# A factorization layer on one core: the 4x2x3 scheme for two more outer products, a fourth output tile and output sums by adding DMAs

## The chip, the cores and the metric

The kernel runs on one core of one Trainium2 chip. The metric is device time in microseconds of one execution, from inputs in HBM to the output in HBM. Shown are the median and the range of several executions, and one execution that the hardware profiler recorded.

## The reference

`x` is 1024 x 512, `weight` is 64 x 512 x 512 (embedding e, feature f, model column m), all in float32.

```
out_lin = x @ lin_w.T + lin_b
xv = einsum('bf,efm->bem', x, weight)
zp = einsum('bf,efm->bem', square(x), square(weight))
y  = out_lin + 0.5 * sum(square(xv) - zp, axis=1)     # sum over e
```

Nearly all of the work is `xv`: a matrix product of 1024 x 512 by 512 x 32768, whose results are squared and summed over e. The sum of `zp` over e is x squared times the sum over e of the squared weights, one small matrix product at the end.

## The kernel before, in words

**Groups.** The 512 model columns are cut into 22 groups, two of 16 columns and twenty of 24 (a "full group"). Each group is one matrix product of 1024 x 512 by 512 x (24 x 64).

**Outer products.** A group is computed by the Strassen-Winograd scheme of 2x2 blocks: seven outer products, numbered 1 to 7, instead of eight. Their left sides (sums of blocks of x) stay in the tiles X1 to X7 for the whole run. Their right sides are blocks of the group's weights, `w11`, `w12`, `w21`, `w22`, and sums of them in `T1` and `T2`. These sums and two more into `w12` and `w21` are made by adding DMAs: four per group, each of 768 KB in a full group, issued by GpSimd (`dma_add`, L342). `w22` and `T1` have two copies, for even and odd groups. The plain weight loads are issued by SP, twelve of 384 KB per full group.

**Inner products.** Each outer product is split once more: into 7 inner products of 384 columns, each in two halves of rows, 14 in all (`tree`), or, for those in `HK`, into 20 products of 256 columns by a scheme for 4x2x3 blocks (`wide_tree`). The sums of weights that these need are made by GpSimd into `t0` to `t2`. The inner products go to four pairs of PSUM banks, `b1`, `b3`, `b2_0`, `b2_1`. ScalarE copies a partial result from pair to pair (`copy`, L319), so that later products accumulate onto it; VectorE and GpSimd (`tt`, L309) bring results into the output tiles `oa`, `ob`, `c`. ScalarE squares finished outputs (L326) and VectorE sums them over e into `acc` (L335).

**Output sums.** Outer product 1 goes to `oa`; 6 gives `ob = oa + P6`; 2 is added to `oa`, which is then finished; 7 gives `oa = ob + P7`; 4 gives `c = oa + P4`, finished; 5 is added to both `oa` and `ob`, each of its results twice, and `oa` is finished; 3 is added to `ob`, which is finished.

**Order.** The program is a list of operations, each with the engines that may run it, a cost on each, and the operations whose data or buffers it needs. A planner (`Plan.order`) plays that list once, with latest times counted back from TensorE's work, and so fixes the order of every engine's queue; each engine then runs its queue strictly in order. In the plan an adding DMA costs GpSimd 1 us, lands a fixed time after that, and then takes up SP for its cost:

```
cost = 2.9 * rows / 1024
plan.add({POOL: 1.0}, emit, reads + writes, writes + (token,), land=cost + 2.5)
plan.add({SP: cost}, None, (token,), ())
```

## Time and profile before

| | |
|---|---|
| median of 3 executions | 1427.72 us (1426.12 to 1429.38) |
| the profiled execution's own span, first to last instruction | 1425.4 us (2.3 us under the median) |
| TensorE, VectorE, GpSimd, ScalarE busy | 99%, 79%, 77%, 51% |
| granted TensorE clock | 1.000 |
| matmul instructions | 4680: two for each product of the code |
| DMA | 184.53 MB, mean 129 GB/s |

In the rows of the profile PE is TensorE, PEld its weight loads, DVE VectorE, ACT ScalarE and POOL GpSimd. A row of instruction groups reads: line, engine, operation, output tile <- input tiles, shapes, count | busy us, mean ns of one | idle time of the engine just before them and what ended it. Buffer numbers are left out of names, so X1 to X7 all read X, and `w` is w11, w12 or w21. A row of DMA queues gives packets, MB and the share of 16 DMA engines' time; a row of DMA issues gives the queue that issues, the count, KB each and the median us from issue to landing. In rows of stretches the busy time of each engine and its count are followed by the granted clock, the DMA share and GB/s.

### The profile page before, as it was taken

The numbers are of one execution on the slowest core, as the hardware profiler recorded it, in microseconds if no ns is written. First come the engines' busy times: TensorE is split into PE (matmuls) and PEld (weight loads), VectorE is DVE, ScalarE is ACT, GpSimd is POOL, SyncE is SP. The second block draws the span as 40 slices with busy tenths as digits, with TensorE's granted clock in tenths as the row PEclk, the third lists the DMA queues.
The fourth block names the chain that finished last, engine by engine and source line by source line (L and its number), as shares of the span: only waits on it lengthen the run. The fifth ranks groups of instructions, "written<-read, shape, count | busy, mean of one in ns | idle before, by whom it ended". The sixth has DMA issues, their size and how long they took to land.

```text
span 1425.4 us, 14830 instructions
## 1 busy us (share of the span) xinstructions
PE 1407.8 (99%) x4680; PEld 883.2 (62%) x4680; DVE 1123.7 (79%) x1365; ACT 731.2 (51%) x1048; POOL 1093.3 (77%) x895
## 2 busy tenths in 40 slices
PE   8999999999999999999999999999999999999998
PEld 3887565666656566665656566665656666565653
DVE  2678778796977879697887879687787969778875
ACT  2446545463645646464554646465464646455431
POOL 7897869696787869687776968787686968878670
PEclk9999999999999999999999999999999999999999
DMA  7667636464653646465463645555364646545241
GB/s 237 183 142 177 150 84 160 116 142 109 141 130 95 163 89 162 102 138 135 109 155 86 156 118 133 125 125 136 89 166 102 156 104 143 129 99 133 67 131 61
DMA packets 78893, 184.53 MB, mean 129 GB/s; under 512 B 28064, under 2 KB 29088, under 8 KB 78816
## 3 DMA queue, kind: packets, MB, share of 16 engines
q1 hardware_dynamic: 65488, 115.17, 27.5%
q0 software_dynamic: 12752, 67.38, 25.1%
q10 hardware_dynamic: 576, 1.05, 0.2%
q8 instruction: 38, 0.62, 0.2%
q14 instruction: 39, 0.32, 0.1%
HBM read 127.04 MB, written 6.19 MB: 93 GB/s over the span
## 4 chain that ended last, share of the span: by engine, by line
PE 91%; DVE 6%; issue 1%; DMA 1%; POOL 1%; ACT 0%; SPq 0%; DVEq 0%; POOLq 0%
PE b L356 75%; PE b_r L356 6%; PE b_l L356 6%; DVE acc L335 1%; DVE ob L309 1%; PE b_l L393 1%; DVE oa L309 1%; PE b_r L393 1%; PE b_l L813 1%; PE b_r L813 1%; DVE p L309 1%; DVE w_sum L335 1%; DMA X<-xT 1%; DVE c L309 0%; DMA ob<-lin_wT 0%
## 5 line engine op out<-in xcount | busy, mean ns | idle before, releaser
L356 PE MATMUL b<-t,X 128*128 128x384 f32 (+1 forms) x2144 | 720.9, 476 | 5.1 <-DVE oa L309 3.3
L356 PEld LDWEIGHTS b<-t,X 128*128 128x128 f32 x2144 | 403.2, 190 | 266.9 <-issue 23.2
L356 PE MATMUL b<-w,X 128*128 128x384 f32 (+1 forms) x816 | 276.1, 474 | 0.0
L309 POOL TENSOR_TENSOR t<-w 128x768 f32<-128x768 f32 (+1 forms) x128 | 182.4, 1431 | 119.7 <-PE b_l L356 104.4
L326 ACT ACTIVATE oa<-oa 128x768 f32<-128x768 f32 (+1 forms) x176 | 144.6, 824 | 201.6 <-DVE oa L309 182.9
L356 PEld LDWEIGHTS b<-w,X 128*128 128x128 f32 x816 | 154.6, 190 | 98.3 <-ACT p L319 13.0
L319 ACT COPY p<-b 128x768 f32<-128x768 f32 (+1 forms) x158 | 122.3, 774 | 173.4 <-PE b L356 173.2
L335 DVE TENSOR_REDUCE acc<-oa 128x12 f32<-128x768 f32 (+1 forms) x176 | 158.6, 921 | 39.9 <-ACT oa L326 39.8
L335 DVE TENSOR_REDUCE w_sum<-wsq 128x12 f32<-128x768 f32 (+1 forms) x176 | 158.6, 921 | 27.7 <-ACT wsq L326 27.7
L309 POOL TENSOR_TENSOR t<-w,t 128x384 f32<-128x384 f32 (+1 forms) x136 | 141.9, 1043 | 4.9
L319 ACT COPY b<-b 128x768 f32<-128x768 f32 (+1 forms) x134 | 102.5, 765 | 74.7 <-PE b L356 70.1
L309 DVE TENSOR_TENSOR oa<-b,oa 128x768 f32<-128x768 f32 (+1 forms) x66 | 61.3, 929 | 86.1 <-PE b L356 86.1
L326 ACT ACTIVATE wsq<-w 128x768 f32<-128x768 f32 (+1 forms) x132 | 104.9, 823 | 46.8 <-DMA w<-weight 31.8
L309 POOL TENSOR_TENSOR ob<-ob,p 128x768 f32<-128x768 f32 (+1 forms) x44 | 78.8, 1791 | 22.9 <-DVE p L309 22.9
L326 ACT ACTIVATE c<-c 128x768 f32<-128x768 f32 (+1 forms) x88 | 70.4, 819 | 47.9 <-DVE c L309 46.6
L356 PE MATMUL b<-T,X 128*128 128x384 f32 (+1 forms) x264 | 92.3, 476 | 0.0
L309 POOL TENSOR_TENSOR t<-t,w 128x256 f32<-128x256 f32 (+1 forms) x80 | 90.2, 1202 | 0.0
L309 DVE TENSOR_TENSOR ob<-b,oa 128x768 f32<-128x768 f32 (+1 forms) x66 | 61.3, 929 | 30.0 <-PE b L356 30.0
L309 DVE TENSOR_TENSOR p<-b,p 128x768 f32<-128x768 f32 (+1 forms) x88 | 81.5, 926 | 1.1 <-ACT wsq L326 0.6
L326 ACT ACTIVATE ob<-ob 128x768 f32<-128x768 f32 (+1 forms) x88 | 71.0, 826 | 21.6 <-DVE ob L309 14.6
L309 DVE TENSOR_TENSOR oa<-oa,b 128x768 f32<-128x768 f32 (+1 forms) x88 | 81.2, 923 | 0.8
L309 DVE TENSOR_TENSOR ob<-ob,b 128x768 f32<-128x768 f32 (+1 forms) x88 | 80.0, 926 | 2.0 <-PE b L356 1.4
(118 smaller groups left out, 2130.8 us busy)
## 6 DMA issues: line engine op xcount, KB each, us to landing
w<-weight SPq DMA_DIRECT2D x120, 384.0 KB, 3.5
T<-weight SPq DMA_DIRECT2D x40, 384.0 KB, 4.2
w<-T POOLq DMA_DIRECT2D x20, 768.0 KB, 5.8
T1a<-weight SPq DMA_DIRECT2D x20, 384.0 KB, 3.7
w22a<-weight SPq DMA_DIRECT2D x20, 384.0 KB, 3.2
T1a<-weight POOLq DMA_DIRECT2D x10, 768.0 KB, 7.9
T<-T1a POOLq DMA_DIRECT2D x10, 768.0 KB, 7.5
T1b<-weight SPq DMA_DIRECT2D x20, 384.0 KB, 4.5
```

The costliest lines, as they stand in the source:

```text
L309: return f(o.ap, a.ap, b.ap)
L319: return nc.scalar.copy(o.ap, i.ap)
L326: lambda _: nc.scalar.activation(o.ap, i.ap, AF.Square), i.atoms, o.atoms)
L335: nc.vector.tensor_reduce(o, x, axis=AX.X, op=ALU.add)
L356: nc.tensor.matmul(a.ap, b.ap, w.ap, start=start, stop=True, skip_group_check=True)
L393: nc.tensor.matmul(o[j].ap, x.ap[:, ts((g * 2 + j) % (NB // 2), P)], w.ap, start=(k == 0), stop=(k == NK - 1),)
L813: nc.tensor.matmul(z.ap, view(xe[h, k // KH])[:, k % KH, ts((g * 2 + j) % (NB // 2), P)], reg("w2_sum", k * M, M).ap, start=(k == 0), stop ...
```

## The change

- The 4x2x3 scheme is used for outer products 1, 6 and 7 (`HK`) in full groups, where only 1 had it. Its sums are written in another form, with seven operations on GpSimd instead of eight.
- There is a fourth output tile, `od`; `c` is now `oc`. Outer product 5 goes to `od` alone, 7 to `oc`, 2 to `oa`, 3 to `ob`, 4 to `oc`. After outer product 7 the new function `outer_out` issues four adding DMAs: `ob += od` in two halves of rows and then `od += oc` in two halves; `od` is then finished.
- The order of outer products is 1 6 5 7 2 3 4.
- In 6, 7, 2, 3 and 4 (`EARLY`), the result P5 of `tree` is added to the output as soon as it is there, and no copy of it is kept.
- The three buffers for sums become one space `t` that is filled in turn; the bias uses `od` at the start; the last stage uses other tiles.
- The planner plays the list 24 times; after each time `blame` raises the urgency of what TensorE waited for, and the time with the earliest end is taken. An adding DMA's cost in the plan is 2.4 instead of 2.9 per 1024 elements.

```diff
-ORDER = (1, 6, 2, 7, 4, 5, 3)
-HK = (1,)
+ORDER = (1, 6, 5, 7, 2, 3, 4)
+HK = (1, 6, 7)
+EARLY = (6, 7, 2, 3, 4)
...
+    def order(self):
+        boost, best = defaultdict(float), None
...
+        for _ in range(ROUNDS):
+            done = self.schedule(boost)
+            end = max(o.end for o, e in done if e == PE)
...
+            if best is None or end < best[0]:
+                best = end, done
+            self.blame(done, boost)
+        return best[1]
+
+    def blame(self, done, boost):
...
+        for o, e in done:
+            if e != PE:
+                continue
+            lost = o.end - o.costs[PE] - free
+            free = o.end
+            if lost < 0.05:
+                continue
+            x = slowest(o)
+            for _ in range(CHAIN):
+                if x is None or x.engine == PE:
+                    break
...
+                boost[x.n] += PUSH * max(lost, 0.2)
...
-            o.latest = latest
+            o.latest = latest - boost[o.n]
...
-    make("oa", 4 * WIDE)
-    make("ob", 4 * WIDE)
-    make("c", 4 * WIDE)
+    for o in ("oa", "ob", "oc", "od"):
+        make(o, 4 * WIDE)
...
-        cost = 2.9 * rows / 1024
+        cost = 2.4 * rows / 1024
         plan.add({POOL: 1.0}, emit, reads + writes, writes + (token,), land=cost + 2.5)
         plan.add({SP: cost}, None, (token,), ())
...
+    def outer_out(g):
+        iw = GROUPS[g] // 2 * E
+        for o, i in (("ob", "od"), ("od", "oc")):
+            for k in range(2):
+                x, y = (reg(z, 2 * k * WIDE, iw, (WIDE, 2)) for z in (o, i))
+                dma_add(x.ap, y.ap, 2 * iw, y.atoms, x.atoms)
+        for m in range(4):
+            finish(g, 5, reg("od", m * WIDE, iw), m, 0)
...
-    ADDEND = {6: "oa", 2: "oa", 7: "ob", 4: "oa", 3: "ob"}
-    TARGET = {1: "oa", 6: "ob", 2: "oa", 7: "oa", 3: "ob", 4: "c"}
+    ADDEND = {6: "oa", 2: "oa", 7: "ob", 4: "oc", 3: "ob"}
+    TARGET = {1: "oa", 6: "ob", 5: "od", 2: "oa", 7: "oc", 3: "ob", 4: "oc"}
...
         product(5, "b3", True)
-        copy(small(p5), whole("b3"))
+        if i in EARLY:
+            leave(3, "b3")
+        else:
+            copy(small(p5), whole("b3"))
         product(3, "b3", False)
...
+            if i == 7:
+                outer_out(g)
```

Three places in the queues, each from a full group in the middle of the run. First GpSimd's queue before, from the sum into w21, which outer product 4 needs, to the sum into w12 for the next group; t0 to t2 are the sums of weights, DMA rows are the adding DMAs, and the words in brackets are the semaphores that the row waits for (DMASW: an adding DMA, DMAHW: a load).

```order
L346 DMA w21_71<-T2_76 128x1536 [waits PE_49]
L309 TENSOR_TENSOR t0_80<-T1a_74 128x2x384 [waits PE_49]
L309 TENSOR_TENSOR oa_77<-p5_0_83,oa_77 128x2x384 [waits DVE_49,Pool_49]
...
L346 DMA T2_76<-T1b_75 128x1536 [waits DMAHW6_49,DMAHW5_49,DMASW4_49]
L309 TENSOR_TENSOR t1_81<-w22a_72,t1_81 128x384 [waits Pool_49]
L309 TENSOR_TENSOR oa_77<-oa_77,ob_78 128x2x384 [waits DVE_49]
...
L346 DMA w12_70<-w22b_73 128x1536 [waits DMAHW4_49,DMAHW7_49,DMAHW0_49,Activation_49]
```

Between the first two adds stand eight operations on tiles, between the second and third five; no two adds are neighbours. Now the same queue of the change, from behind outer product 7's last sums to the first sum for outer product 4 (t from w21):

```order
L403 DMA ob_78<-od_80 128x1536 [waits DVE_49]
L403 DMA ob_78<-od_80 128x1536 [waits Pool_49]
L366 TENSOR_TENSOR t_81<-w22b_73,t_81 128x384 [waits Pool_49]
L403 DMA w21_71<-T2_76 128x1536 [waits PE_49]
L366 TENSOR_TENSOR t_81<-w22b_73,t_81 128x384 [waits Pool_49]
L366 TENSOR_TENSOR t_81<-w11_69 128x768 [waits DMAHW5_49,DMAHW4_49]
L403 DMA w12_70<-w22a_72 128x1536 [waits DMAHW2_49,DMAHW6_49,DMAHW1_49,Activation_49]
L403 DMA od_80<-oc_79 128x1536 [waits DMASW6_49]
L403 DMA od_80<-oc_79 128x1536 [waits DMASW7_49,DVE_49]
L366 TENSOR_TENSOR t_81<-t_81,w11_69 128x512 [waits PE_49,Pool_49]
L366 TENSOR_TENSOR t_81<-w21_71 128x2x384 [waits DMASW0_49]
```

The sums into w21 and w12 now stand among the four new adds, six adds with three operations between them; DMASW6 and DMASW7 are the two `ob` adds, DMASW0 is the one into w21. Then TensorE's queue of the change where outer product 4 (X4) begins, with products of outer product 3 (X3) between:

```order
L413 MATMUL b1<-w21_71,X4_65 128x384 [waits DMASW0_49,DVE_49]
L413 MATMUL b1<-w21_71,X4_65 128x384
L413 MATMUL b3<-t_81,X4_65 128x384 [waits DVE_49,Pool_49]
L413 MATMUL b3<-t_81,X4_65 128x384
L413 MATMUL b2_0<-t_81,X3_64 128x384 [waits DVE_49]
L413 MATMUL b2_0<-t_81,X3_64 128x384
L413 MATMUL b2_1<-t_81,X4_65 128x384 [waits Activation_49,Pool_49]
L413 MATMUL b2_1<-t_81,X4_65 128x384
L413 MATMUL b3<-w21_71,X4_65 128x384 [waits DVE_49]
L413 MATMUL b3<-w21_71,X4_65 128x384
L413 MATMUL b1<-w21_71,X4_65 128x384 x2
L413 MATMUL b2_1<-t_81,X4_65 128x384 [waits DVE_49]
```

and VectorE's queue at that place, where the results of outer product 4 in b3 and b2_1 leave for `oc`:

```order
L392 TENSOR_REDUCE acc1_89<-ob_78 128x2x6 [waits Activation_49]
L366 TENSOR_TENSOR oc_79<-b3,oc_79 128x2x384 [waits DMASW2_49,PE_49]
L366 TENSOR_TENSOR ob_78<-b2_0,ob_78 128x2x384 [waits PE_49]
L366 TENSOR_TENSOR oc_79<-b2_1,oc_79 128x2x384 [waits DMASW3_49,PE_49,Activation_49]
L392 TENSOR_REDUCE acc1_89<-ob_78 128x2x6
```

DMASW2 and DMASW3 are the two `od` adds. TensorE's second pair of products into b3 waits for the first of these VectorE operations, and its pair into b2_1 in the last row for the third. Before, no row of a group in the middle of the run has VectorE wait for an adding DMA.

## The prediction

> **What bounds the kernel now.** I read the page first, its busy shares and its chain of waits, then the chain in order of time over the steady part, then the DMA queues, and last the queue of GpSimd around one group.

> ```profile
> span 1425.4 us, 14830 instructions
> PE 1407.8 (99%) x4680; PEld 883.2 (62%) x4680; DVE 1123.7 (79%) x1365; ACT 731.2 (51%) x1048; POOL 1093.3 (77%) x895
> PE 91%; DVE 6%; issue 1%; DMA 1%; POOL 1%; ACT 0%; SPq 0%; DVEq 0%; POOLq 0%
> ```

> TensorE is 91% of the chain that ended last. In the middle of the run the chain is TensorE alone, in order of time:

> ```profile
> 506.96 3.87 PE b L356 x12
> 510.83 1.73 PE b_l L356 x8
> ...
> 516.87 49.10 PE b L356 x152
> ...
> 569.92 3.87 PE b L356 x12
> ...
> 632.88 3.87 PE b L356 x12
> ```

> The same piece returns every 62.96 us (506.96, 569.92, 632.88): the period of one full group, with nothing but matmuls in it. A matmul instruction of 384 columns takes 49.10/152 = 0.323 us there, one of 256 columns 1.73/8 = 0.216 us, and every product in the code is two such instructions. So the time falls with TensorE's work and with nothing else, as long as no operand or bank comes late.

> **Scheme 4x2x3 for 6 and 7.** A full group's outer product costs 14 products of 384 columns, 14 x 2 x 0.3230 = 9.044 us; in the new scheme 20 of 256 columns, 20 x 2 x 0.2163 = 8.650 us. Two of them in 20 groups: 40 x 0.394 = 15.8 us less. The period would be 62.2 us.

> **Smaller operations on the other engines.** By the lists of both kernels VectorE's tensor operations go from 620 of 768 elements, 122 of 512 and 80 of 256 to 400, 284 and 280. One takes:

> ```profile
> L309 DVE TENSOR_TENSOR oa<-b,oa 128x768 f32<-128x768 f32 x60 | 57.2, 953 | 82.6 <-PE b L356 82.6
> L309 DVE TENSOR_TENSOR oa<-b_l,p 128x512 f32<-128x512 f32 x40 | 25.9, 686 | 7.8 <-PE b_l L356 7.8
> L309 DVE TENSOR_TENSOR oa<-b_r,p 128x256 f32<-128x256 f32 x60 | 25.3, 422 | 35.2 <-PE b_r L356 33.2 <-ACT oa L319 1.2 <-ACT p L319 0.4
> L309 POOL TENSOR_TENSOR t<-w 128x768 f32<-128x768 f32 x60 | 113.3, 1888 | 107.5 <-PE b_l L356 104.4 <-DMA w<-T 3.0 <-PE b L356 0.2
> L309 POOL TENSOR_TENSOR t<-t,w 128x256 f32<-128x256 f32 x40 | 34.4, 860 | 0.0
> L346 POOL DMA_DIRECT2D w<-T x22 | 19.0, 865 | 71.5 <-PE b L356 71.5
> ```

> VectorE: -220 x 0.953 + 162 x 0.686 + 200 x 0.422 = -14 us, so it stays near 79%: dropping the double addition of outer product 5 pays for the smaller pieces. GpSimd loses 160 of 768 elements (-302 us) and 80 of 384 (about 1.1 us each, between the two rows, -88), and gains 102 of 512 (about 1.4 each, between the two rows as well, +143), 290 of 256 (+249) and 88 issues of adding DMAs (+76): about +80 us, 77% becomes 82%. ScalarE gains short copies on its 51%. None is full, so I cost these at nothing; what hides them is TensorE's 62 us a group, and the price if that cover fails is the second rival.

> **The two output sums by DMA.** This term decides. Per full group four adding DMAs of 768 KB are new (`ob += od` and `od += oc`, each in two halves); four were there (the sums of weights).

> ```profile
> q1 hardware_dynamic: 65488, 115.17, 27.5%
> q0 software_dynamic: 12752, 67.38, 25.1%
> w<-T POOLq DMA_DIRECT2D x20, 768.0 KB, 5.8
> T<-T1a POOLq DMA_DIRECT2D x10, 768.0 KB, 7.5
> ```

> All adding DMAs run in the one software queue. It holds 25.1% of 16 engines over 1425.4 us, 358 us for 67.38 MB: an add of 768 KB (0.786 MB) costs 4.2 us **of all 16 engines**. The shortest median from issue to landing is 5.8 us, so 1.6 us of it are start and completion. A weight load of 384 KB costs likewise 27.5% x 1425.4 x 0.393/115.17 = 1.34 us. Over a group that is 8 x 4.2 + 12 x 1.34 = 50 of 62 us: busy, not full. But where the adds stand matters. Before, they were spread, each alone:

> ```profile
> 779.82 0.87 POOL L346 DMA_DIRECT2D w<-T  x1 [3.69 <-PE b L356]
> 793.60 0.84 POOL L346 DMA_DIRECT2D T<-T1b  x1
> 801.19 0.85 POOL L346 DMA_DIRECT2D w<-w22b  x1
> 816.98 0.83 POOL L346 DMA_DIRECT2D T1a<-weight  x1
> ```

> In the changed order six stand in one stretch between outer product 7 and outer product 4: `ob`, `ob`, `w21` (for 4), `w12` (the next group's, moved ahead from behind the sums for 1), `od`, `od`. GpSimd issues them in that order, and the planner gives each its own fixed landing time, without a queue behind one another. Whether they queue is read from stretches with one add alone, two adds (of 512 KB) close together, and one add beside two weight loads:

> ```profile
> 718.30:722.30 4.00, 4.00 (x14) 2.38 (x13) 3.34 (x4) 2.11 (x3) 3.07 (x2) 1.00 0.99 195
> 52.50:58.70 6.20, 6.12 (x29) 5.10 (x28) 5.10 (x8) 3.57 (x6) 5.45 (x8) 1.00 1.02 191
> 135.40:142.90 7.50, 7.50 (x25) 4.48 (x24) 4.90 (x6) 1.66 (x4) 1.81 (x1) 1.00 0.97 205
> ```

> The last columns are DMA share and GB/s. One add alone fills 0.99 of the 16 engines for its 4 us; two take 6.2 us at 1.02, and one with two loads 7.5 us at 0.97, against 4.2 + 2 x 1.34 = 6.9 by the costs above. So the share stays at 1 and the stretch grows: there is no room beside an add, and queued adds must follow each other.

> Now the time line of one group, zero at the end of TensorE's last matmul of outer product 7. The last reader of `ob` on VectorE ends at about 1.0 (one operation of 0.953 for outer product 2 is ahead of it, then 0.686 us of its own). GpSimd issues the first `ob` add at 1.1, the second 0.87 later. `w21` waits until outer product 2's six first products are through (6 x 0.645 = 3.9), which is early enough to stand third without a gap; `w12` follows two sums of t. So the first `od` add is the fifth of an unbroken row and lands at 1.1 + 1.6 + 5 x 4.2 = 23.7. Five weight loads fall into the same stretch by the order of SP's queue (two halves of w22, two of T2, which wait for the `w21` add, one of w21): up to 5 x 1.34 = 6.7 more, 30.4.

> Who needs it: outer product 4 writes its first result (P5, which now leaves early) into `oc`, and VectorE may not overwrite `oc` before the `od` add has read it. TensorE's product 3 of outer product 4 accumulates onto the same bank b3, so it waits for that VectorE operation. By TensorE's order 30 products of 384 columns lie between zero and it: 30 x 2 x 0.323 = 19.4 us. VectorE ends at 23.7 + 0.95 = 24.6 without loads, 31.3 with all five: TensorE stands for 5.2 to 11.9 us. The second `od` add lands 4.2 us after the first, and the next result into b2 waits for it; four products (2.6 us) are run meanwhile, so 1.6 us are added. Together **6.8 to 13.5 us a group**. Behind the waiting VectorE operation are outer product 3's last result and the reductions for `ob`; behind TensorE's wait is everything. I take 10: between no load in the way and all of them, nearest to two or three loads. The next thing that could be late, T2 += T1 for the next group's 6, then lands near 38 us, while product 6 begins near 42 since TensorE has lost those 10 us; I cost it at nothing, and if it is late by its own 4.2 us the upper bound holds it.

> Nineteen full groups have this row: 190 us. The last has neither the `w12` add nor next loads: the `od` add is fourth, 1.1 + 1.6 + 16.8 + 0.95 = 20.5 against 19.4, with the second 2.7 us, say 2.5. In the two first groups an add is 512 KB, 2.8 us; `od` is fourth and TensorE's 30 products take 30 x 2 x 0.216 = 13: 1.1 + 1.6 + 11.2 + 0.7 = 14.6 without loads, some 17 with them; with the second add about 4 each, 8 together.

> **Other edits.** The new order 1 6 5 7 2 3 4 leaves one outer product between 2 and 4, as before (7 stood there), and two (4 and 1) for T2's reload where it had four; the time line above holds both. The t space, the moved bias and the repeated scheduling issue no other transfers; the last changes only orders, read above. What stalls TensorE had before outside the steady part, I leave as they are; a gain from better orders there is bounded by the 9% of the chain that is not PE, 128 us, of which head and tail stay, so I take none.

> **Sum.** 1425.4 - 15.8 + 190 + 2.5 + 8 = 1610.1 for the profiled execution; the median of the runs shown is 1427.72, 2.3 more than that span: **1612 us**. The bounds 6.8 and 13.5 give 19 x 6.8 = 129 (1552) and 19 x 13.5 = 257 (1679). A smaller price per add (3.9, if start and end lie over one another) takes 1.5 us per group off the lower one, 1523.

> **Rivals.** First, on the other side: **the adds do not queue up**. If each lands 5.8 us after its issue whatever stands ahead, `ob` lands at 6.9, `od` at 13.6, VectorE is done at 14.5 and TensorE, due at 19.4, never waits: 1427.7 - 15.8 = 1412. It decides where an add behind another costs under 2.9 us instead of 4.2 (1.1 + 1.6 + 4.2 + 4x + 0.95 = 19.4, with no load between). For it speaks that the median landings of before, each add mostly alone, are 5.8 to 7.9 us; against it the share of 0.99 with one add. Somewhat under a microsecond of stall a group would make it no change. [...] Chance 0.11, and 0.03 for no change.

> Second, slower by another way: **the results of the 4x2x3 trees leave too slowly**. Each passes some ten short results through VectorE and ScalarE between matmuls of 0.43 us; if three of them come late by one VectorE operation of 0.686 us in both new trees, a group loses 4.1 us: 1412 + 82 = 1494. It decides where VectorE's answer takes longer than the matmuls of the neighbouring product that the order puts between. Against it: the one such tree of before costs the chain nothing visible in the 62.96 us. Chance 0.05.

> **How the numbers follow.** Forecast 0.81, second rival 0.05, first 0.11, no change 0.03. About 0.2% is what a measurement here can tell from no change: faster 0.11, same 0.03, slower 0.86. The range 1500 to 1680 holds the forecast with both bounds of the stall and the cheaper add; outside are the first rival and most of the second.

> **What would show it.** Right: DMA share near 1 for over 20 us after outer product 7; landings of `ob<-od` and `w<-T` growing to about 10 us and of `od<-oc` to 12 to 20; VectorE's `oc<-b,oc` waiting for the DMA `od<-oc` in every full group, and TensorE's weight loads for VectorE's `oc`; a period of 70 to 75 us in place of 62.2. Wrong: `od<-oc` landing within 8 us of issue, a period of 62 to 63, or a waiting TensorE whose releaser is VectorE without a DMA behind it.

## The result and the profile after

The changed kernel takes 1666.93 us (median, 1665.14 to 1669.49), against 1427.65 us for the kernel before measured beside it: a ratio of 1.168, 95% interval 1.166 to 1.170. The forecast was slower, 1612 us, with a range of 1500 to 1680; the time lies inside, 55 us above the forecast. The profiled execution has a span of 1664.8 us, 239.4 more than before's.

First the page of the changed kernel: the span and the busy shares, the shares of the chain that ended last, the DMA queues (packets, MB, share of 16 engines), then two groups and the DMA issues with their median us to landing. In the names of all rows `b` is a PSUM bank of a product of 384 columns, `b_l` and `b_r` are banks in the 4x2x3 products.

```profile
span 1664.8 us, 16601 instructions
PE 1482.9 (89%) x5160; PEld 985.1 (59%) x5160; DVE 1113.0 (67%) x1509; ACT 782.4 (47%) x1225; POOL 1146.7 (69%) x1149
q0 software_dynamic: 26448, 134.49, 42.5%
q1 hardware_dynamic: 65488, 115.17, 20.9%
PE 40%; DMA 39%; POOL 13%; ACT 3%; issue 3%; DVE 1%; SPq 0%; POOLq 0%; ACTq 0%; DVEq 0%
...
L366 DVE TENSOR_TENSOR oc<-b,oc 128x768 f32<-128x768 f32 (+1 forms) x88 | 81.6, 931 | 191.7 <-DMA od<-oc 190.8
L413 PE MATMUL b<-w,X 128*128 128x384 f32 (+1 forms) x576 | 237.0, 556 | 103.0 <-DVE oc L366 97.2
...
ob<-od POOLq DMA_DIRECT2D x40, 768.0 KB, 7.8
od<-oc POOLq DMA_DIRECT2D x40, 768.0 KB, 18.0
T<-weight SPq DMA_DIRECT2D x40, 384.0 KB, 11.3
w<-T POOLq DMA_DIRECT2D x20, 768.0 KB, 11.6
```

TensorE's share of the chain fell from 91% to 40%, and DMA, 1% before, now has 39%. The price of an add held: 42.5% of 1664.8 us for 134.49 MB is 4.14 us for 0.786 MB. What changed is the landing: `w<-T` went from 5.8 to 11.6 us, the `od` adds land 18.0 us after their issue, and T2's reload went from 4.2 to 11.3. VectorE's writes into `oc` stand idle 190.8 us for the `od` adds, and behind them TensorE 97.2 us in one group of instructions alone.

One full group of the changed kernel, around the row of adds. The stretches give busy time of each engine, and at the end the granted clock, the DMA share and GB/s; the first is the whole row of adds, the second its end.

```profile
857.40:882.90 25.50, 20.00 (x54) 10.96 (x55) 16.41 (x19) 8.84 (x11) 13.01 (x12) 0.90 1.03 229
871.00:883.00 12.00, 7.66 (x18) 4.11 (x18) 3.21 (x4) 1.17 (x3) 3.48 (x4) 0.79 1.03 252
```

The DMA engines are full for 25.5 us on end (share 1.03), and in that time the granted clock of TensorE is 0.90, in the second stretch 0.79. The same group in the time lines of ScalarE, VectorE and TensorE (start, us, instruction, idle before it and its releaser):

```profile
855.41 1.71 ACT L383 ACTIVATE wsq<-w 128x768 f32<-128x768 f32 x2 [3.65 <-DMA w<-weight]
856.28 0.95 DVE L392 TENSOR_REDUCE w_sum<-wsq 128x12 f32<-128x768 f32 x1 [2.15 <-ACT wsq L383]
857.15 0.95 DVE L366 TENSOR_TENSOR oa<-b,oa 128x768 f32<-128x768 f32 x1
...
878.17 0.96 DVE L366 TENSOR_TENSOR oc<-b,oc 128x768 f32<-128x768 f32 x1 [5.78 <-DMA od<-oc]
883.08 0.96 DVE L366 TENSOR_TENSOR oc<-b,oc 128x768 f32<-128x768 f32 x1 [3.08 <-DMA od<-oc]
```

```profile
852.48 0.59 PE L413 MATMUL b_r<-t,X 128*128 128x256 f32 x2
858.16 1.56 PE L413 MATMUL b<-t,X 128*128 128x384 f32 x4 [1.22 <-DVE oa L366]
862.62 2.74 PE L413 MATMUL b<-t,X 128*128 128x384 f32 x8
870.71 4.14 PE L413 MATMUL b<-t,X 128*128 128x384 f32 x12 [0.15 <-POOL t L366]
879.19 5.49 PE L413 MATMUL b<-w,X 128*128 128x384 f32 x8 [4.34 <-DVE oc L366]
```

Outer product 7 ends at 853.07. The first `od` add lands at 878.1, VectorE writes `oc` at once, and TensorE, idle for 4.34 us, goes on at 879.19. Its next eight matmuls take 5.49 us, where at 862.62 eight of the same form take 2.74 at the full clock: twice as long. And at 858.16 there is a wait that the forecast did not have: TensorE waits for `oa<-b,oa`, which stood in VectorE's queue behind a reduction (`w_sum`), which waited for ScalarE's square, which waited for a weight load.

The chain of waits in order of time carries the period, 857.24 to 931.14, 73.9 us. Up to 898.98 there is no matmul in it; from there to 926.56 it is TensorE alone:

```profile
857.24 11.52 DMA w<-T
869.16 14.02 DMA T<-weight
883.71 6.72 DMA T<-T1a
890.59 1.81 POOL t L366
892.49 4.28 POOL t L366 x3
...
931.14 11.59 DMA w<-T
```

So in this group the stop of 4.34 us at `oc` is not on the chain. The chain runs over the add into `w21`, T2's reload, which waits for that add, then T2 += T1 and the sums `t`; TensorE waits another 0.50 us for these at 898.98. Of the 20 full groups, ten have the `od` adds on the chain and nine have T2's reload as here. Two late paths of nearly the same length leave the one row of adds, and shortening one of them alone gains only up to where the other ends.

**An account of TensorE's time.** For each matmul I took the time from the end of the one before it to its own end, less its duration at full rate, and put the rest to what released it. TensorE's work is 1396.3 us before and 1381.1 after, 15.2 less. What it lost beside its work is 18.3 before and 273.1 after, 254.8 more. The two make 239.6, within 0.2 us the difference of the spans. Of the 273.1 us after: waits for VectorE's `oc` 120.2 (100.6 of them in 21 stops of 4.8 us, at the first `od` add), the half clock (time lost while the granted clock is 0.5, see the last section) 46.1, VectorE's `oa` 31.4, GpSimd's sums `t` 27.1, ScalarE's copy `b_l` 10.9, the rest, 37, is small pieces, gaps under 0.2 us between matmuls and short waits. The same account is used for each run below.

### The profile page after: what moved, and what is told of

Same layout as the page of the kernel before. It is cut to its first block, busy times and chain, and to the rows that moved or that the text cites. A ratio compares the mean times of both kernels' runs of the same rounds, so it can differ in the third digit from the quotient of the medians.

```text
span 1664.8 us, 16601 instructions
## 1 busy us (share of the span) xinstructions
PE 1482.9 (89%) x5160; PEld 985.1 (59%) x5160; DVE 1113.0 (67%) x1509; ACT 782.4 (47%) x1225; POOL 1146.7 (69%) x1149
## 3 DMA queue, kind: packets, MB, share of 16 engines
q0 software_dynamic: 26448, 134.49, 42.5%
q1 hardware_dynamic: 65488, 115.17, 20.9%
## 4 chain that ended last, share of the span: by engine, by line
PE 40%; DMA 39%; POOL 13%; ACT 3%; issue 3%; DVE 1%; SPq 0%; POOLq 0%; ACTq 0%; DVEq 0%
PE b L413 17%; DMA od<-oc 13%; POOL t L366 11%; PE b_r L413 11%; PE b_l L413 11%; DMA T<-weight 8%; DMA w<-T 7%; DMA ob<-od 5%; DMA T<-T1a 2%; DMA T<-T1b 2%; POOL ob L403 1%; ACT od L383 1%; PE b_r L880 1%; PE b_l L880 1%; POOL X L366 1%
## 5 line engine op out<-in xcount | busy, mean ns | idle before, releaser
L413 PE MATMUL b<-t,X 128*128 128x384 f32 (+1 forms) x1504 | 527.2, 483 | 44.6 <-DVE oa L366 25.8
L413 PEld LDWEIGHTS b<-t,X 128*128 128x128 f32 x1504 | 279.3, 193 | 239.7 <-POOL t L366 36.3
L413 PE MATMUL b<-w,X 128*128 128x384 f32 (+1 forms) x576 | 237.0, 556 | 103.0 <-DVE oc L366 97.2
L366 POOL TENSOR_TENSOR t<-w 128x768 f32<-128x768 f32 (+1 forms) x88 | 163.2, 1855 | 75.5 <-DMA w<-T 42.5
L366 DVE TENSOR_TENSOR oc<-b,oc 128x768 f32<-128x768 f32 (+1 forms) x88 | 81.6, 931 | 191.7 <-DMA od<-oc 190.8
L366 POOL TENSOR_TENSOR t<-t,w 128x256 f32<-128x256 f32 (+1 forms) x200 | 199.5, 1040 | 2.6 <-PE b_l L413 0.5
L413 PE MATMUL b_l<-t,X 128*128 128x256 f32 x720 | 191.3, 381 | 3.1 <-POOL t L366 2.9
L413 PE MATMUL b_r<-t,X 128*128 128x256 f32 x600 | 173.3, 388 | 18.4 <-POOL t L366 8.0
L413 PEld LDWEIGHTS b_l<-t,X 128*128 128x128 f32 x720 | 136.1, 190 | 34.5 <-POOL t L366 7.2
L413 PEld LDWEIGHTS b_r<-t,X 128*128 128x128 f32 x600 | 109.6, 190 | 72.9 <-issue 18.1
L383 ACT ACTIVATE ob<-ob 128x768 f32<-128x768 f32 (+1 forms) x88 | 71.5, 820 | 61.1 <-DVE ob L366 60.9
L413 PE MATMUL b_r<-w,X 128*128 128x256 f32 x400 | 99.4, 380 | 0.0
L366 POOL TENSOR_TENSOR t<-t,T 128x256 f32<-128x256 f32 (+1 forms) x100 | 92.8, 945 | 3.2
## 6 DMA issues: line engine op xcount, KB each, us to landing
ob<-od POOLq DMA_DIRECT2D x40, 768.0 KB, 7.8
od<-oc POOLq DMA_DIRECT2D x40, 768.0 KB, 18.0
T<-weight SPq DMA_DIRECT2D x40, 384.0 KB, 11.3
w<-T POOLq DMA_DIRECT2D x20, 768.0 KB, 11.6
T1a<-weight POOLq DMA_DIRECT2D x10, 768.0 KB, 6.8
```

Of the source, the lines that this page charges most:

```text
L366: return f(o.ap, a.ap, b.ap)
L383: lambda _: nc.scalar.activation(o.ap, i.ap, AF.Square), i.atoms, o.atoms)
L413: nc.tensor.matmul(a.ap, b.ap, w.ap, start=start, stop=True, skip_group_check=True)
```

## Experiments

The theory: the six adding DMAs in a row pass one after another; the `od` adds land too late, and through VectorE's `oc` TensorE stands still, then runs at half clock. The rivals: the 4x2x3 trees leave too slowly, or something else of the new order. A run given with a ratio is the median of four or more executions, the others are one execution each. In the two runs with smaller adds the order of every queue stays; in all others the planner makes a new one, so that more can move than the lines shown.

**Small output adds.** The four output adds move 16 of 128 partitions, in the same order and with the same waits; the sums of the other partitions are missing from the output.

```diff
-                dma_add(x.ap, y.ap, 2 * iw, y.atoms, x.atoms)
+                dma_add(x.ap[0:16], y.ap[0:16], 2 * iw, y.atoms, x.atoms)
```

> [...] Theory (the adds queue up in one ring, 4.2 us each): the waits of VectorE and TensorE for the od adds go (120 us) and with them the half-clock stretches (46 us): 1667 - 166 = about 1500, down to 1420 if the other late operands hang on the adds too. Rival (the 4x2x3 trees and their sums are late by themselves): over 1600.

1496.34 us, as the theory had it. Here are its DMA queue and issues, and what VectorE and GpSimd still wait for (us in total, times, longest):

```profile
q0 software_dynamic: 15696, 75.77, 34.7%
ob<-od POOLq DMA_DIRECT2D x40, 96.0 KB, 4.9
od<-oc POOLq DMA_DIRECT2D x40, 96.0 KB, 11.0
```

```profile
DVE oc L366 <- DMA od<-oc: 8.4, 12, 2.7
POOL T L403 <- DMA T<-weight: 61.9, 13, 5.6
DVE w_sum L392 <- ACT wsq L383: 36.0, 22, 2.6
```

170 us go with seven eighths of these adds: VectorE's wait for `od` goes from 190.8 to 8.4 us, TensorE's waits for `oc` from 120.2 to 4.1, the half clock from 46.1 to 3.4. But a small add is not a free one: the queue's time falls from 707.5 us (42.5% of 1664.8) to 518.6 (34.7% of 1494.6), 2.2 us for each of the 80 adds of full groups, with the eight smaller ones of the first groups counted by their bytes; so one with an eighth of the bytes still costs some 1.9, by this estimate. And 102.7 us of loss are left: GpSimd's sums `t` 42.3, VectorE's `oa` 28.5. These two did not go with the bytes.

**Without the new 4x2x3 products.** The changed kernel with the scheme for outer product 1 only.

```diff
-HK = (1, 6, 7)
+HK = (1,)
```

> The changed kernel with the 4x2x3 scheme for outer product 1 alone; fourth tile, adding DMAs, order and planner as changed. Theory: the adds stand in one row as before, so the stall stays and TensorE has 15 us more work: 1640 to 1690. Rival (the trees are late): the loss goes with them, 1430 to 1450.

1660.42 us. The slowdown stays without the new trees. It moves, though. TensorE waits now for GpSimd's sums:

```profile
PE b L413 <- POOL t L366: 109.0, 21, 6.9
w<-T POOLq DMA_DIRECT2D x20, 768.0 KB, 15.3
```

With another order of the sums the row of adds is felt at another operand: nearly all of this wait follows the sum from `w21`, whose add stands behind four others in the group around 860 us and lands 15.3 us (median) after its issue instead of 11.6. The period hardly changes. The half clock is there again: the granted clock is 0.957 over the run, and 54.7 us are lost by it.

**The next group's `w12` add behind the `od` adds.**

```diff
-            dma_add(o.ap, reg(i, 0, n).ap, n, reg(i, 0, n).atoms, o.atoms)
+            after = (('odq', g - 1, 0), ('odq', g - 1, 1)) if which == 3 else ()
+            dma_add(o.ap, reg(i, 0, n).ap, n, reg(i, 0, n).atoms, o.atoms, after)
...
-                dma_add(x.ap, y.ap, 2 * iw, y.atoms, x.atoms)
+                dma_add(x.ap, y.ap, 2 * iw, y.atoms, x.atoms, ((o + 'q', g, k),))
```

> The changed kernel with one more dependence in the plan: the next group's add into w12 is issued after the two od adds, so these are fourth and fifth in the row instead of fifth and sixth. [...] Rival (trees): no change, 1660 to 1670.

1592.32 us, 75 less, just past the end of the theory's range (1540 to 1590: some 80 us from `od` landing 4.2 us earlier, the rest from the half clock). By the account TensorE's waits for `oc` fall from 120.2 to 33.3 us and the half clock from 46.1 to 18.5, and GpSimd's sums `t` rise from 27.1 to 84.2: a good part of what the `od` adds give back is lost at the sums of weights. The moved add is the smaller part of that. Followed back, 34 us of the stops (19 of them) end at the sum from `w21`, whose add lands as before (11.5 us after its issue, 11.6 in the changed kernel); in the group around 904 us TensorE's new order asks for that sum four matmuls earlier. Some 13 us end at the moved `w12` add.

```profile
DVE oc L366 <- DMA od<-oc: 68.9, 31, 6.4
PEld b L413 <- POOL t L366: 70.4, 51, 5.0
```

**The `w12` add smaller, not moved.** It moves 16 of 128 partitions and stays in its place, so those sums are incomplete.

```diff
-            nc.gpsimd.dma_start(o, i, accum_op=ALU.add)
+            nc.gpsimd.dma_start(o[0:16] if few else o, i[0:16] if few else i, accum_op=ALU.add)
...
-            dma_add(o.ap, reg(i, 0, n).ap, n, reg(i, 0, n).atoms, o.atoms)
+            dma_add(o.ap, reg(i, 0, n).ap, n, reg(i, 0, n).atoms, o.atoms, which == 3)
```

> The changed kernel, same order and waits, but of the next group's adding DMA into w12 only 16 of 128 partitions are moved (those sums are left incomplete, so the output lacks them). One add of about 4.2 us leaves the row ahead of the od adds without any other instruction moving. Theory: the wait of VectorE's oc for od (7.8 us twice per group) falls by some 4 us, and most idle stretches of TensorE become too short for half clock, so the 21 waits of 4.8 us and the 46 us of half clock go almost wholly; the add T2+=T1 comes 4 us earlier too, so that TensorE's waits for POOL t, 84 us in the run with the w12 add moved behind, stay near 27 to 45. Sum 1667 - 100 - 40 = about 1525 (1500 to 1560). Rival (the price is in the number of adds of the output only, T2 is late for another reason, its weight loads): 1580 to 1600, as with the add moved behind, with POOL t again at 80. Second rival (od is late because of its own loads): within 15 of 1667.

1612.47 us: outside all three ranges, and a miss in size. The landings say why:

```profile
q0 software_dynamic: 23984, 119.81, 41.1%
ob<-od POOLq DMA_DIRECT2D x40, 768.0 KB, 8.1
od<-oc POOLq DMA_DIRECT2D x40, 768.0 KB, 15.4
```

The `od` adds land 2.6 us earlier, not 4.2, because the small add still costs nearly half of a full one: the queue gives back 707.5 - 662.0 = 45.5 us over the 20 adds of full groups and two smaller ones, 2.1 for a full one, as in the first run. The time fell by 54 us, 2.9 for each of 19 groups, of which the account has 37 us at `oc` and 12 at the half clock; the sums `t` stay at 23.3. So with every order kept the time follows the landing of the `od` adds, 2.9 us for 2.6. The rise of `t` in the run before came with its new order. The half clock did not go, against the theory: 22 half-rate stretches are left, behind shorter stops (last section).

**A later need for `od`.** Outer product 4 no longer lets its P5 leave early.

```diff
-EARLY = (6, 7, 2, 3, 4)
+EARLY = (6, 7, 2, 3)
```

> The changed kernel, but outer product 4 no longer lets its fifth product leave early, so the first result of outer product 4 that needs od is one product later; nothing else of the order of the adds is changed. Theory (the wait is for the od adds, at a fixed time after outer product 7): TensorE gains one product of 4 matmul groups, 2.6 to 4 us per group of 19, and some idle stretches fall under 4 us and keep the full clock: 1667 - 50 to - 75 = 1590 to 1617. Rival (the first add was only a part and the second add, 3.6 us behind, decides): 1640 to 1670. Second rival (the later leave moves the same wait into the following outer product): 1660 to 1690.

1672.65 us, within 6 of the changed kernel. The theory's gain of 50 to 75 us did not come. The time lies 3 us over the first rival's range and inside the second's, so the trace has to decide. In the same group of this run, where the `w21` add is issued at 863.80, VectorE and TensorE read:

```profile
889.61 0.96 DVE L366 TENSOR_TENSOR oc<-b,oc 128x768 f32<-128x768 f32 x1 [8.47 <-DMA od<-oc]
890.62 2.93 PE L413 MATMUL b<-t,X 128*128 128x384 f32 x4 [6.61 <-DVE oc L366]
```

There is now one stop of 6.61 us, at the second `od` add, in place of one of 4.34 at the first. After the issue of `w21`, VectorE's write behind the second add starts 25.81 us later here (889.61 - 863.80) and 25.84 in the changed kernel (883.08 - 857.24). The stop is in outer product 4 still, and not in the next one: the second add sets the pace, the first rival of this run. It also says what the half clock is worth: in the changed kernel the eight slow matmuls end just after the second add has landed (884.68 against 882.96), so a part of the 46 us would have been spent waiting for it anyway.

**A plan that knows the queue.** The planner is told that adds pass one after another at 4.2 us each.

```diff
+                    if o.serial:
+                        ring = max(now + 1.4, ring) + o.serial
+                        o.end = ring + 0.4
...
+        plan.ops[-1].serial = 4.2 * rows / 1536
```

> The changed kernel, whose planner now lets each adding DMA begin only when the one before it is through (4.2 us per 768 KB, 1.4 us from issue to begin, 0.4 us to land); nothing else is changed, the order comes out of it. Theory: the plan puts the od adds ahead of the next group's w12 as in the run with w12 late and looks after T2 as well, but ob, ob, w21, od still follow one another: 1520 to 1590. Rival (trees late by themselves): 1640 to 1670.

1675.69 us: a miss. The `od` adds did come earlier in their queue (12.2 us to landing instead of 18.0), and TensorE's waits for `oc` halved to 55 us. The lateness moved to the weight loads, whose delay beside adds the plan does not know (those of T2 and `w22` land 10.5 to 11.0 us after their issue, 3.1 to 4.2 in the kernel before):

```profile
ACT wsq L386 <- DMA w<-weight: 253.8, 47, 9.8
POOL T L406 <- DMA T<-weight: 182.2, 21, 10.4
PE b_r L417 <- ACT b_l L379: 82.6, 19, 5.9
```

ScalarE's squares of weights wait 253.8 us for their loads, and the copies `b_l` that stand behind them in its queue release TensorE 82.6 us late. A better model of one transfer did not help while the loads beside it landed that late.

**The output sums on VectorE and GpSimd.** All else of the change stays.

```diff
-                dma_add(x.ap, y.ap, 2 * iw, y.atoms, x.atoms)
+                for m in (2 * k, 2 * k + 1):
+                    x, y = (reg(z, m * WIDE, iw) for z in (o, i))
+                    tt(x, x, y)
```

> The changed kernel with the two output sums made by VectorE or GpSimd (eight operations of 768 elements per full group) in place of the four adding DMAs. Theory: the adds of weights stand alone again, so no od wait and no half clock; eight operations are 7.6 us of VectorE per group, 152 us in all, 1113 + 152 = 1265 of some 1450: 1430 to 1500. Rival (trees late by themselves): 1600 or more.

1468.96 us, ratio 1.031 (1.028 to 1.034), as the theory had it. So the DMA form of the two sums costs 198 us, and no half clock is left (granted clock 1.000). The rest of the change costs 42 us still. Its busy shares and its largest waits of TensorE:

```profile
PE 1412.0 (96%) x5160; PEld 966.8 (66%) x5160; DVE 1106.0 (76%) x1509; ACT 795.0 (54%) x1225; POOL 1362.9 (93%) x1237
PE b_l L413 <- ACT b_l L376: 25.2, 19, 1.7
```

GpSimd is at 93%. The waits for `oa` (3.0) and `t` (3.4) are gone here: they belong to the stretch with the full DMA engines, not to the trees.

**The 4x2x3 scheme alone,** the kernel before with one line changed.

```diff
-HK = (1,)
+HK = (1, 6, 7)
```

> The kernel before with the 4x2x3 scheme for 1, 6 and 7 and nothing else: no fourth tile, no output adds by DMA, old order and one play of the plan. Theory: TensorE's 15 us are gained, less what the trees lose by themselves (nothing to 60 us): 1412 to 1470. Rival (trees late by themselves): 1500 to 1650.

1448.94 us, ratio 1.016 (1.014 to 1.017), where TensorE's smaller work alone would give 1411. The account has 55.0 us of loss for 18.3 before.

```profile
PE 1411.5 (98%) x5160; PEld 967.4 (67%) x5160; DVE 1130.2 (78%) x1527; ACT 799.0 (55%) x1248; POOL 1368.2 (95%) x1279
PEld b_r L356 <- POOL t L309: 14.3, 18, 0.8
PEld b L356 <- DVE ob L309: 14.1, 23, 0.8
```

No wait is long; they are short ones at many places, 17.9 us of them gaps without a wait. GpSimd goes from 77% to 95% of the span: here the small tensor operations fall to GpSimd, and VectorE stays at 78%.

**The same with the repeated scheduling.** The edit is the line above and the new `order`, `blame` and `schedule`.

> The kernel before with the 4x2x3 scheme for 1, 6 and 7 and the repeated scheduling of the change, without fourth tile, adds and new order. Theory: without output adds the repeated scheduling takes back some of the 37 us that the trees lost when the plan was played once (1449): 1415 to 1440. Rival (the loss is the engines' own, no order mends it): 1445 to 1455.

1458.23 us, ratio 1.022 (1.021 to 1.024): a miss, slower than with the list played once. The planner's repeated search takes the order that ends first in its own model, and on the chip that order lost 65.4 us beside the work instead of 55.0. Which of its costs is wrong was not looked for.

**The scheme for 1 and 7 only,** with the repeated scheduling.

```diff
-HK = (1,)
+HK = (1, 7)
```

> The kernel before with the repeated scheduling and the 4x2x3 scheme for outer products 1 and 7 only (not 6), no fourth output tile and no output sums by DMA. TensorE's work falls by about two thirds of 15.2 us, 10 us, from 1396. Theory (the trees of two 4x2x3 products next to each other, 1 then 6, are what leaves late): with 6 back on the old scheme the loss beside the work is 20 to 30 us instead of 65, so 1412 to 1425. Rival (each 4x2x3 product costs its own 1.2 us or more per group wherever it stands): 1435 to 1450.

1434.98 us, ratio 1.006 (1.004 to 1.008), at the low end of the rival. TensorE's work is 1388.7, 7.6 less than before, and the loss 32.9; with the repeated scheduling alone (next run) it is 14.4. So the second such product costs 18.5 us of waits for its 7.6, and the third, 6, right behind 1, costs 65.4 - 32.9 = 32.5 for the next 7.6. Neither text is borne out cleanly: each product has its price, as the rival says, and the last one a higher one. Whether that is its place behind 1, as the theory says, or that it is the third, is not shown: 1 and 6 without 7 was not run. The largest wait of TensorE in this run is 11.6 us, in 22 stops of at most 2.8 us for ScalarE's `b_l`.

**The repeated scheduling alone.**

> The kernel before with the repeated scheduling alone. Theory: of the 18 us that TensorE loses in the kernel before, some 8 lie in full groups and can be mended: 1418 to 1427. Rival (repeated scheduling trades real for planned gains): 1430 or more.

1423.85 us, ratio 0.9987 (0.9977 to 0.9996): the one version that beats both kernels, by 0.13%. TensorE is 96% of its chain instead of 91%.

```profile
PE 96%; POOL 1%; DMA 1%; DVE 1%; issue 0%; ACT 0%; SPq 0%; DVEq 0%; ACTq 0%; POOLq 0%
```

Put in a row, with medians: before 1426.5; the 4x2x3 products +22; the repeated scheduling on top of them +9; all other edits (fourth tile, order, early P5, the other form of the 4x2x3 sums and what goes with them), with the output sums on engines, +11; the two sums by adding DMAs +198.

## Why the prediction was right, and where it was off

**4x2x3 saves 15.8 us.** TensorE's work fell by 15.2. Right.

**Smaller operations cost nothing.** Wrong as a step. In the changed kernel it is hidden, since GpSimd, relieved of the output sums, is at 69%. But alone the scheme loses 37 us more than before beside its work, and the whole change without DMA sums 55 more. The forecast added up busy time and found no engine full, from an estimate for GpSimd that held only with the sums on DMA. The second rival had priced the waits at 82 us, with a chance of 0.05, for late results of the trees. What the runs show in its place is many short waits with GpSimd at 93 to 95%; which of the two causes it, the short pieces or the fuller engine, the runs do not tell apart.

**Adds follow one another at 4.2 us; `od` is fifth.** Right: 4.14 us by the queue's share, and the first `od` add landed 878.1 - 853.07 = 25.0 us after outer product 7, forecast 23.7 to 30.4. The first rival, adds that overlap, is ruled out: by the semaphores of the trace the six adds of the group shown land at 860.29, 864.24, 868.76, 873.35, 878.08 and 882.96, 4.0 to 4.9 us apart. Against the 5.8 us from issue to landing that the forecast took for an add alone, the row hides 0.9 to 1.8 us of each, about the start and completion (1.6 us by the forecast), and none of its 4 us of the engines.

**The stall of 10 us a group.** The place was right: the wait of `oc<-b,oc` for the `od` add stands in every full group, and TensorE behind it. But it is on the chain in ten of the 20 full groups only; in nine the chain goes over T2's reload instead, which the forecast had costed at nothing. The size was less. The forecast took 190 + 2.5 + 8 = 200.5 us; the waits for `oc` are 120.2, and 166.3 with the half clock, some 8.3 for each of 20 groups. Two terms were too large. Fewer loads got in the way than I took: 25.0 is 1.3 above the row without loads, the 10 stood for about 3 us of loads. And TensorE came some 2 us later to the stall than planned, since it had waited for `oa` before. The term "1.6 for the second add" was put on top of the first; the run with the later need shows that the second add alone sets the pace, so that moving the first need gains nothing.

**Costed at nothing and not nothing.** VectorE's `oa`, 31.4 us: the weight loads also land late (5.4 us instead of 3.5), and a square, a reduction and then `oa` stand behind them in strict order. The forecast had queues on GpSimd and SP, and only followed the late adds, not the late plain loads. GpSimd's `t`, 27.1 us: T2 += T1 landed 37.4 us after outer product 7 (883.71 + 6.72 - 853.07), forecast 38, but behind it GpSimd still had four sums, 6.1 us, before outer product 6's first operands were there, which the step left out. The `b_l` copies are 10.9, the small pieces some 19 more than before. These make 88 us. With the 166 they are the 254.8 us more loss than before, where the forecast had 200.5: 54 us, which is the error.

**The half clock**, 46.1 us, was in no step. It is worked out below. So the nearness of the forecast is in part luck: the waits at `oc` were 80 us less than it took, and the half clock with what it costed at nothing 135 us more.

**The signs** named beforehand all came: share 1.03 for 25.5 us, landings of 7.8 and 11.6 for `ob<-od` and `w<-T` (about 10 forecast), 18.0 for `od<-oc` (12 to 20), a period of 73.9 us (70 to 75).

## What to carry to other kernels

Here six adds with loads between them kept the DMA share at 1.03 for 25.5 us and landed 4.0 to 4.9 us apart. Treat such a transfer as an instruction of a queue like any other: put its whole row on a time line with its neighbours, add the loads that fall into the same stretch, and follow each late landing through every in-order queue behind it, not only the first. Here two paths behind the same row were about equally late. Before work is moved from an engine to the DMA, ask whether the engine was on the path at all: here TensorE was 91% of the chain, and the two sums cost 198 us there and none of the engines they relieved had been the bound. And price a stop of TensorE with the clock that follows it: in the group shown eight matmuls behind the stop of 4.34 us took 5.49 us instead of 2.74.

## What the runs showed that was not expected

**TensorE's granted clock fell to 0.50 around stops of a few microseconds.** Before, the granted clock was 1.000; after, 0.965. In one group of the changed kernel:

```profile
804.96 5.22 PE L413 MATMUL b<-w,X 128*128 128x384 f32 x8 [4.33 <-DVE oc L366]
```

```profile
795.00:804.96 9.96, 5.35 (x17) 2.59 (x15) 3.87 (x6) 2.68 (x4) 5.25 (x5) 0.90 1.04 243
804.96:810.20 5.24, 5.24 (x9) 2.89 (x10) 2.19 (x3) 1.48 (x2) 0.76 (x2) 0.54 0.96 288
810.20:813.00 2.80, 2.71 (x10) 1.44 (x9) 2.80 (x4) 2.80 (x5) 2.22 (x4) 1.00 0.79 141
```

```profile
420.53:423.94 3.41, 1.47 (x5) 0.68 (x4) 2.29 (x3) 2.40 (x4) 1.41 (x3) 1.00 0.97 385
423.94:427.35 3.41, 3.39 (x8) 2.44 (x8) 3.41 (x5) 3.41 (x5) 1.58 (x3) 0.50 1.08 225
```

In the first TensorE is busy for 1.47 of 3.41 us, 57% idle; in the second, 3.39 us busy, the clock is 0.50. I counted all such windows of the nine traces that have half-rate stretches, without start and end. Of those at full rate, all 115 that were idle for 60% or more were followed by a half-rate one, 20 of 49 between 50 and 60%, and none of the 3662 below. A half-rate window was followed by full rate in all 134 cases with under 15% idle, and in none of the 62 with 20% or more.

These are counts of this case's traces; what sets the clock is not shown by them.

**An add with an eighth of the bytes cost nearly half.** 768 KB take 4.14 us of the queue, 96 KB (16 of 128 partitions) some 1.9, an estimate from the shares of the first run. Whether the fixed part is in the rows, the partitions or the start of each DMA was not tried.
